# A graph layer on one core: A^T by block loads and score rows through DRAM, in place of TensorE transposes

## The chip, the cores and the metric

The kernel runs on one NeuronCore of a Trainium2 chip. The metric is the device time of one execution in microseconds (us), lower is better; the median of several runs counts. One execution was also recorded by the hardware profiler, and all views below come from it. PE is TensorE, PEld its weight load, DVE VectorE, ACT ScalarE, POOL GpSimd, SP the engine that only issues DMAs.

## The reference

There are 128 graphs of 128 nodes with 512 features, a weighted adjacency matrix A for each, and two layers.

```python
h = relu(layernorm(x))
sj, si = (h @ Wv + bv) @ aw[:512], (h @ Wv + bv) @ aw[512:]      # one number per node
e = leaky_relu(sj[:, None, :] + si[:, :, None] + ab, 0.2)
alpha = A * exp(e)
T = alpha / (sum(alpha, -1) + 1e-12)
x = x + relu(h @ Wk[0] + (T @ h) @ Wk[1] + (T @ T @ h) @ Wk[2] + bk.sum(0))

h = relu(layernorm(x))
q, k = split(h @ Wqk);  v = h @ Wv1
w = mask * sum(q * (A @ (k * mask)), -1) / sqrt(512)             # one number per node
x = x + softmax(w over the nodes)[:, :, None] * v
```

Two vectors of one number per node are needed along the free axis: sj, which is added to every row of e, and w, whose maximum and sum over all nodes are needed in every partition. A^T is needed as the stationary operand of the second layer's aggregation.

## The kernel before

A node is a partition. The kernel takes the graphs in pairs (`G = 2`), 64 of them (`NP`), with p counting the pairs; all data are fp32. The weights are folded in a setup: `score_matrix` makes one matrix of Wq and Wk, `attention_weights` folds Wv and aw into two vectors (`u_bc`), so that the scores are two weighted row sums of h.

Each layer multiplies the pair of graphs with its weights by one level of Strassen's scheme, seven products in place of eight: `strassen0` for layer 0 (the three hops stacked, L356 to L385) and `strassen1` for layer 1 (L387 to L409). Products are matmuls with a stationary operand of 128x128 (L346) into three banks of a PSUM pool of four; DVE adds the banks together between them. Results of other TensorE work go to a second pool of four banks (`ps_t`, tile `pt`).

A column of one number per node is turned into a row, the same in all partitions, by `spread` (L95 to L97): a TensorE transpose of the column broadcast to 128x128. A^T is a TensorE transpose too (L298), read out of PSUM by ACT with the mask as scale (L302). For h the kernel already goes another way: `by_blocks` (L258 to L266) stores h in DRAM and reads it back by four DMAs, so that 32x32 blocks lie in the right place, and `transposed` (L268 to L272) has DVE transpose every 32x32 block. SP issues these DMAs, and all others in the loop.

The steps of pair p, in the order of the text:

- `strassen0(p, steps)`: seven products; after the second, `steps[0]` runs `begin(p+1)` (block transposes of h into the operand x), `attention(p+1)` (L274 to L302: the score row, z, exp, the weighted sum with A, t = T, and A^T) and `end()`, which runs `finish` of pair p-2 (L426 to L445: the softmax over w, the last sum and the store). After the fourth product, `steps[1]` runs `t_transposed(p+1)` (L304 to L315: T^T, and (TT)^T by a matmul; ACT copies both out, L310 and L314).
- `propagate(p+1)`: T h and T T h, transposed (L325), copied out by ACT (L327).
- `norm_relu` of the first layer's result (L235 on ACT), its `by_blocks`.
- `strassen1(p-1)`, then `aggregate(p-1)` (L411 to L424: A k by L417 and the weighted row sum w by L420 on DVE).
- `prepare0(p+1)` and the block transposes and sums of layer 1's operand.
- `norm0(p+2)`, which loads pair p+3 (`load`, L68 to L73) and normalizes, and `score_sums(p+2)` (L248 to L256: four row sums on DVE, L255).

The instructions are not issued in just this order. The framework's planner orders each engine's queue ahead of the run, by the order of the text as priority and by its own costs of when an operand will be there; each queue then runs strictly in its order, and semaphores make it wait. A tile name with several buffers rotates; a new tile waits until the last reader of the old one is done. GpSimd's queue holds only a few set-up instructions.

Of the kernel before, what the change touches and what calls it, by code (L numbers as in the profile page):

```python
# [8 lines left out]
FP = mybir.dt.float32  # L9
# [6 lines left out]
def kernel(  # L16
# [27 lines left out]
    G = 2  # L44
# [20 lines left out]

    xg, ag = {}, {}

    def load(p):  # L68
        s = slice(p * G, (p + 1) * G)
        xg[p] = loads.tile([P, G, D], FP, name="xg")  # L70
        nc.sync.dma_start(xg[p], x[s].rearrange("b n d -> n b d"))
        ag[p] = loads.tile([P, G, N], FP, name="ag")
        nc.sync.dma_start(ag[p], adj[s].rearrange("b n m -> n b m"))  # L73


# [19 lines left out]
    def spread(dst, col):  # L95

        nc.tensor.transpose(dst, col.to_broadcast([P, P]), ident)  # L97
# [140 lines left out]

    H, HV, S, X, SX, AT, T, TT, X1, H2, X2, SX2 = ({} for _ in range(12))

# [7 lines left out]
    def score_sums(p):  # L248

        h = H[p]  # L250
        s = S[p] = small.tile([P, G, 2], FP, name="s")
        for j in range(G):
            for a in range(2):
                junk = front.tile([P, D], FP, name="junk", bufs=1)
                nc.vector.scalar_tensor_tensor(junk, h[:, j, :], 1.0, u_bc[:, a, :], op0=OP.mult,  # L255
                                               op1=OP.mult, accum_out=s[:, j, a:a + 1])  # L256

# [10 lines left out]
    def transposed(hv, dst):  # L268

        for j in range(G):  # L270
            nc.vector.transpose(dst[:, j].rearrange("p f (n b) -> p f n b", n=Q),  # L271
                                hv[:, j].rearrange("p n (f a) -> p f n a", f=Q))  # L272

    def attention(p):  # L274

        a, s = ag.pop(p), S.pop(p)
        pz = ps_t.tile([P, DC, P], FP, name="pt")
        for j in range(G):
            spread(pz[:, j, :], s[:, j, 0:1])
        z = front.tile([P, G, N], FP, name="z", bufs=1)  # L280
        for j in range(G):
            nc.vector.tensor_scalar(z[:, j, :], pz[:, j, :], s[:, j, 1:2], cz, op0=OP.add, op1=OP.add)
        nc.vector.scalar_tensor_tensor(z, z, 0.2, z, op0=OP.mult, op1=OP.max)
        ex = front.tile([P, G, N], FP, name="ex")
        nc.scalar.activation(ex, z, AF.Exp)
# [5 lines left out]
        nc.vector.reciprocal(d[:, 1], d[:, 0])  # L291
        t = T[p] = front.tile([P, G, N], FP, name="t")
        for j in range(G):
            nc.vector.tensor_scalar(t[:, j, :], ex[:, j, :], d[:, 1, j:j + 1], None, op0=OP.mult)

        pa = ps_t.tile([P, DC, P], FP, name="pt")
        for j in range(G):
            nc.tensor.transpose(pa[:, j, :], a[:, j, :], ident)  # L298
        AT[p] = front.tile([P, G, N], FP, name="aT", bufs=3)
        for j in range(G):  # L300
            b = p * G + j
            nc.scalar.activation(AT[p][:, j, :], pa[:, j, :], AF.Copy, scale=maskT[:, b:b + 1])  # L302

    def t_transposed(p):  # L304

        t, tt = T.pop(p), front.tile([P, G, 2, N], FP, name="tt")
        pt = ps_t.tile([P, DC, P], FP, name="pt")
# [48 lines left out]
    def strassen0(p, steps):  # L356
# [13 lines left out]
        steps[0]()  # L370
        product(bc, 7, True)
        product(bb, 5, False)
        nc.vector.tensor_add(s[:, 3], b, s[:, 0])
        nc.vector.tensor_add(hb[:, 1, HD:], c, s[:, 3])
        steps[1]()
        product(ba, 2, False)
        nc.vector.tensor_add(hb[:, 0, :HD], a, lo)
        product(bb, 3, False)
        nc.vector.tensor_add(hb[:, 0, HD:], b, s[:, 0])
# [6 lines left out]

    def strassen1(p):  # L387

# [12 lines left out]
        nc.vector.tensor_add(s[:, 2], b, s[:, 0])  # L401
        nc.vector.tensor_add(o[1][1], c, s[:, 2])
        product(a, 2, False)
        nc.scalar.copy(o[0][0], a)
# [6 lines left out]
    def aggregate(p, yv):  # L411

        h2, at = H2.pop(p), AT.pop(p)
        w = small.tile([P, 6, G], FP, name="w")
        for j in range(G):
# [6 lines left out]
                wscale[:, b:b + 1], yv[:, j, :, 0, :], op0=OP.mult, op1=OP.mult,  # L422
                accum_out=w[:, 0, j:j + 1])
        return w  # L424

    def finish(p, yv, w):  # L426

        pw = ps_t.tile([P, DC, P], FP, name="pt")
        for j in range(G):
            spread(pw[:, j, :], w[:, 0, j:j + 1])  # L430
        nc.vector.tensor_reduce(w[:, 1], pw[:, :G, :], AX.X, OP.max, negate=True)
        for j in range(G):
# [43 lines left out]
    for p in range(NP + 1):  # L476
        if p < NP:
            if p + 1 < NP:
                n = p + 1
                steps = (lambda: (begin(n), attention(n), end()), lambda: t_transposed(n))  # L480
            else:
                steps = (end, lambda: None)
            strassen0(p, steps)
            if p + 1 < NP:
                propagate(p + 1)
        else:
            end()
# [5 lines left out]
        if p < NP:  # L493
            H2[p] = norm_relu(X1[p], "h2", late["p"])
            hv2 = by_blocks(H2[p])
        if p > 0:
            yv = strassen1(p - 1)
            w = aggregate(p - 1, yv)
        if p + 1 < NP:
            prepare0(p + 1)  # L500
        if p > 0:
            ends.append((p - 1, yv, w))
        if p < NP:
# [4 lines left out]
            SX2[p] = left_sums(a, late["p"], "sx2", [1, HD])  # L508
        if p + 2 < NP:
            norm0(p + 2)  # L510
            score_sums(p + 2)
    end()
# [25 lines left out]
```

## Time and profile before

| | us |
|---|---|
| median of three runs | 2420.17 (2419.18 to 2420.50) |
| the profiled execution | 2420.37 |
| its span, first to last instruction | 2418.3 |
| one pair of graphs in the steady part | 36.70 |
| granted TensorE clock | 0.998 of full |

| group of instructions | count | mean ns |
|---|---|---|
| L346 products, 128x256 / 128x512 | 5376 / 1792 | 380 / 592 to 598 |
| L97 transposes of s, of w | 128, 128 | 276, 274 |
| L298 transposes of A | 128 | 275 |
| L271 DVE block transposes of 128x512 | 256 | 688 |
| L255 DVE score sums, 128x512 | 256 | 689 |
| L282 z from the score row in PSUM, 128x128 | 128 | 402 |
| L431 maximum over the row in PSUM, 128x256 | 64 | 414 |
| L302 ACT copy of A^T from PSUM, 128x128 | 128 | 363 |

The time of a matmul is from its start to its modelled end, and neighbours overlap, so the distance from start to start tells what one takes out of the time. A row of the stretches of time (used below) gives the stretch in us, its length, then for PE, PEld, DVE, ACT and POOL the busy us with the number of instructions, then the granted clock, the DMA engines' busy share and GB/s. DMA issues are not counted as busy. In the steady part the DMA engines are busy some 30% of the time; a DMA of 128 KB issued by SP takes some 3 us from issue to landing (`ag` 3.0, `hv` 3.3), one of 512 KB 3.1 to 3.6.

### The profile page before, as it was taken

To read this page: it belongs to the slowest core of one execution; us is meant where nothing else is said; L and a number is where in the kernel's file an instruction comes from. 1 tells how busy PE (TensorE), PEld (TensorE's weight loads), DVE (VectorE), ACT (ScalarE), POOL (GpSimd) and SP (SyncE) were. 2 spreads that over 40 slices of the span, in tenths; PEclk is the share of its full clock that TensorE was granted. 3 is DMA by queue.
4 is the path that set the end of the run, shared out by engine and by line. 5 is a ranking of instruction groups with operands and counts; after the bars stand their busy time and mean duration, and the time that the engine had idled before them with its cause. 6 is when DMAs were issued, how large, how long until landed. Compare 5 with 4: busy or idle time off the path is not lost.

```text
span 2418.3 us, 27245 instructions
## 1 busy us (share of the span) xinstructions
PE 2378.8 (98%) x9289; PEld 1694.5 (70%) x9289; DVE 1786.8 (74%) x4768; ACT 650.5 (27%) x1557; POOL 0.7 (0%) x6
## 2 busy tenths in 40 slices
PE   6999999999999999999999999999999999999997
PEld 4777677677676676776776776776766767767764
DVE  6777777777777777777777777777777777777764
ACT  3222222222222222223222222222222222232221
POOL 0000000000000000000000000000000000000000
PEclk9999999999999999999999999999999999999999
DMA  7233233233133233232332332332332332323311
GB/s 219 82 84 101 81 92 101 66 106 101 64 109 93 71 101 95 77 101 88 85 101 81 92 100 65 108 100 64 108 93 72 101 95 78 100 87 86 97 52 52
DMA packets 236986, 220.48 MB, mean 91 GB/s; under 512 B 14384, under 2 KB 170160, under 8 KB 236848
## 3 DMA queue, kind: packets, MB, share of 16 engines
q1 hardware_dynamic: 232624, 216.65, 30.5%
q10 hardware_dynamic: 4224, 2.10, 0.3%
q8 instruction: 73, 1.20, 0.2%
q14 instruction: 65, 0.53, 0.1%
HBM read 118.03 MB, written 100.66 MB: 90 GB/s over the span
## 4 chain that ended last, share of the span: by engine, by line
PE 96%; DVE 2%; DMA 1%; issue 0%; ACT 0%; SPq 0%; DVEq 0%; ACTq 0%
PE pm L346 79%; PE pt L325 9%; PE pt L417 4%; PE pt L97 1%; PE pt L313 1%; PE pt L298 1%; PE pt L309 1%; DMA bk_bc<-in_L_gnn_bk_dram 0%; DMA hd<-h 0%; DVE st L220 0%; DMA hv<-hd 0%; DMA w<-in_L_gnn_Wqk_dram 0%; DMA xg<-in_x_dram 0%; DVE x L271 0%; PE pm L208 0%
## 5 line engine op out<-in xcount | busy, mean ns | idle before, releaser
L346 PE MATMUL pm<-t,sx 128*128 128x256 f32 x2304 | 518.6, 380 | 1.4 <-DVE sx L333 1.4
L346 PEld LDWEIGHTS pm<-t,sx 128*128 128x128 f32 x2304 | 433.4, 190 | 57.4 <-DVE sx L333 2.0
L346 PE MATMUL pm<-b,x 128*128 128x256 f32 x1536 | 363.0, 380 | 0.0
L346 PE MATMUL pm<-f,sx 128*128 128x512 f32 x768 | 344.8, 598 | 0.3
L346 PEld LDWEIGHTS pm<-b,x 128*128 128x128 f32 x1536 | 282.6, 191 | 59.3 <-issue 29.6
L327 ACT COPY x<-pt 128x512 f32<-128x512 f32 x256 | 148.7, 581 | 500.6 <-PE pt L325 500.6
L346 PEld LDWEIGHTS pm<-f,sx 128*128 128x128 f32 x768 | 141.6, 191 | 193.7 <-issue 154.4
L346 PE MATMUL pm<-e,x 128*128 128x512 f32 x512 | 242.5, 596 | 6.5 <-DVE x L271 6.5
L325 PE MATMUL pt<-tt,h 128*128 128x256 f32 x1024 | 231.5, 379 | 0.0
L325 PEld LDWEIGHTS pt<-tt,h 128*128 128x128 f32 x1024 | 194.9, 190 | 26.2
L255 DVE SCALAR_TENSOR_TENSOR junk<-h,u_bc 128x512 f32<-128x512 f32 x256 | 176.4, 689 | 7.8 <-ACT h L235 0.9
L346 PE MATMUL pm<-b,sx 128*128 128x256 f32 x768 | 176.5, 379 | 0.0
L346 PE MATMUL pm<-t,x 128*128 128x256 f32 x768 | 176.2, 379 | 0.0
L235 ACT ACTIVATE h<-x,rs 128x512 f32<-128x512 f32 x128 | 97.2, 806 | 289.9 <-PE pt L417 277.1
L271 DVE STREAM_TRANSPOSE x<-hv 128x512 f32<-128x512 f32 x256 | 166.4, 688 | 6.6 <-DMA hv<-hd 5.7
L346 PEld LDWEIGHTS pm<-e,x 128*128 128x128 f32 x512 | 97.8, 191 | 102.8 <-issue 92.3
L346 PEld LDWEIGHTS pm<-t,x 128*128 128x128 f32 x768 | 146.2, 190 | 19.6
L346 PEld LDWEIGHTS pm<-b,sx 128*128 128x128 f32 x768 | 146.0, 190 | 19.5
L406 DVE TENSOR_TENSOR yv<-pm,s 128x512 f32<-128x512 f32 x64 | 44.3, 692 | 128.5 <-PE pm L346 128.5
L235 ACT ACTIVATE h<-xg,rs 128x512 f32<-128x512 f32 x128 | 97.2, 806 | 119.8 <-DVE rs L232 119.8
L417 PE MATMUL pt<-h,aT 128*128 128x512 f32 x256 | 120.5, 593 | 0.5 <-ACT h L235 0.5
L346 PE MATMUL pm<-e,sx 128*128 128x512 f32 x256 | 120.3, 592 | 0.0
(101 smaller groups left out, 2511.3 us busy)
## 6 DMA issues: line engine op xcount, KB each, us to landing
hd<-h SPq DMA_DIRECT2D x128, 512.0 KB, 3.1
hv<-hd SPq DMA_DIRECT2D x512, 128.0 KB, 3.3
xg<-in_x_dram SPq DMA_DIRECT2D x64, 512.0 KB, 3.6
out_dram<-x SPq DMA_DIRECT2D x64, 512.0 KB, 3.1
ag<-in_adj_dram SPq DMA_DIRECT2D x64, 128.0 KB, 3.0
w<-in_L_gnn_Wqk_dram ACTq DMA_DIRECT2D x8, 256.0 KB, 5.0
b<-in_L_gnn_Wk_dram SPq DMA_DIRECT2D x8, 256.0 KB, 3.4
wv_sb<-in_L_gnn_Wv_dram SPq DMA_DIRECT2D x4, 256.0 KB, 5.3
```

Source lines behind the costliest of these rows:

```text
L97: nc.tensor.transpose(dst, col.to_broadcast([P, P]), ident)
L235: nc.scalar.activation(h[:, j, :], src[:, j, :], AF.Relu, bias=rs[:, 1, j:j + 1], scale=rs[:, 0, j:j + 1])
L255: nc.vector.scalar_tensor_tensor(junk, h[:, j, :], 1.0, u_bc[:, a, :], op0=OP.mult, op1=OP.mult, accum_out=s[:, j, a:a + 1])
L271: nc.vector.transpose(dst[:, j].rearrange("p f (n b) -> p f n b", n=Q), hv[:, j].rearrange("p n (f a) -> p f n a", f=Q))
L298: nc.tensor.transpose(pa[:, j, :], a[:, j, :], ident)
L309: nc.tensor.transpose(pt[:, j, :], t[:, j, :], ident)
L313: nc.tensor.matmul(pt[:, j, :], t[:, j, :], tt[:, j, 0, :], start=True, stop=True)
L325: nc.tensor.matmul(pt[:, c].rearrange("p k n -> p (k n)"), h[:, j, at:at + P], tt[:, j].rearrange("p k n -> p (k n)"), start=True, stop=True)
L327: nc.scalar.copy(X[p][:, 1:3, j, kh].rearrange("p k c n -> p c k n"), pt)
L346: nc.tensor.matmul(bank[:, :r.shape[-1]], left[i][:, k, c * P:(c + 1) * P], r, start=(first and at == 0), stop=(at == len(chunks) - 1), sk ...
L406: nc.vector.tensor_add(o[0][1], b, s[:, 0])
L417: nc.tensor.matmul(pa, at[:, j, :], h2[:, j, :], start=True, stop=True)
```

## The change

It touches how two kinds of rows and A^T come about, and where some steps stand.

- A^T: `load` also reads A by four DMAs issued by GpSimd into `agb`, with the 32x32 blocks in their transposed places; `attention` has DVE transpose the blocks into `aT`, and ACT scales `aT` in place.
- Rows: the new `spread_pair` takes a 32-column tile whose first columns are the values of the two graphs. DVE transposes its 32x32 blocks, GpSimd writes the row of each graph to DRAM (two DMAs) and reads both back broadcast to all partitions (one DMA). The score row of pair 0 and the weight row of the last pair keep the TensorE transposes. s and w now live in six fixed 32-column tiles, cleared once.
- Places: `strassen0` has four steps in place of two: `begin` after the second product, `attention` after the third, `end` after the fourth and its sums, `t_transposed` after the fifth. `norm0(p+2)` stands ahead of `strassen1(p-1)`, and `score_sums(p+2)` within it, after the fourth product; the score row's DMAs are issued there, the weight row's where `end` is prepared.
- Buffers: `ex` is the tile `z`, and `t` and `tt` have one buffer each.

```diff
--- before.py
+++ after.py
@@ -63,7 +63,7 @@
 
         return bass.AP(tensor=ap.tensor, offset=ap.offset + offset, ap=[[0, P], [1, n]])
 
-    xg, ag = {}, {}
+    xg, ag, agb = {}, {}, {}
 
     def load(p):
         s = slice(p * G, (p + 1) * G)
@@ -71,6 +71,10 @@
         nc.sync.dma_start(xg[p], x[s].rearrange("b n d -> n b d"))
         ag[p] = loads.tile([P, G, N], FP, name="ag")
         nc.sync.dma_start(ag[p], adj[s].rearrange("b n m -> n b m"))
+        agb[p] = loads.tile([P, G, Q, S32], FP, name="agb", bufs=2)
+        v = adj[s].rearrange("g (q b) (c i) -> c b (g q) i", b=S32, i=S32)
+        for c in range(Q):
+            nc.gpsimd.dma_start(agb[p][c * S32:(c + 1) * S32].rearrange("p g q i -> p (g q) i"), v[c])
 
 
     nc.scalar.preload_act_table_set("natural_log_exp_and_others")
@@ -236,7 +240,10 @@
                                  bias=rs[:, 1, j:j + 1], scale=rs[:, 0, j:j + 1])
         return h
 
-    H, HV, S, X, SX, AT, T, TT, X1, H2, X2, SX2 = ({} for _ in range(12))
+    cols = [const.tile([P, S32], FP, name=f"col{i}") for i in range(6)]
+    for t in cols:
+        nc.gpsimd.memset(t, 0.0)
+    H, HV, S, PZ, X, SX, AT, T, TT, X1, H2, X2, SX2 = ({} for _ in range(13))
 
     def norm0(p):
 
@@ -248,12 +255,13 @@
     def score_sums(p):
 
         h = H[p]
-        s = S[p] = small.tile([P, G, 2], FP, name="s")
+        s = S[p] = cols[p % 3]
         for j in range(G):
             for a in range(2):
                 junk = front.tile([P, D], FP, name="junk", bufs=1)
                 nc.vector.scalar_tensor_tensor(junk, h[:, j, :], 1.0, u_bc[:, a, :], op0=OP.mult,
-                                               op1=OP.mult, accum_out=s[:, j, a:a + 1])
+                                               op1=OP.mult, accum_out=s[:, a * G + j:a * G + j + 1])
+        PZ[p] = spread_pair(s, "pz", p > 0)
 
     def by_blocks(h):
 
@@ -271,17 +279,31 @@
             nc.vector.transpose(dst[:, j].rearrange("p f (n b) -> p f n b", n=Q),
                                 hv[:, j].rearrange("p n (f a) -> p f n a", f=Q))
 
+    def spread_pair(col, name, by_dma):
+
+
+        if by_dma:
+            t = small.tile([P, S32], FP, name=f"{name}t", bufs=1)
+            nc.vector.transpose(t, col)
+            d = dram.tile([G, Q, S32], FP, name=f"{name}d")
+            for j in range(G):
+                nc.gpsimd.dma_start(d[j], t[j::S32])
+            dst = front.tile([P, G, N], FP, name=name, bufs=1)
+            nc.gpsimd.dma_start(dst.rearrange("p g n -> p (g n)"), bcast(d, 0, G * N))
+            return dst
+        pz = ps_t.tile([P, DC, P], FP, name="pt")
+        for j in range(G):
+            spread(pz[:, j, :], col[:, j:j + 1])
+        return pz[:, :G]
+
     def attention(p):
 
-        a, s = ag.pop(p), S.pop(p)
-        pz = ps_t.tile([P, DC, P], FP, name="pt")
-        for j in range(G):
-            spread(pz[:, j, :], s[:, j, 0:1])
+        a, s, pz = ag.pop(p), S.pop(p), PZ.pop(p)
         z = front.tile([P, G, N], FP, name="z", bufs=1)
         for j in range(G):
-            nc.vector.tensor_scalar(z[:, j, :], pz[:, j, :], s[:, j, 1:2], cz, op0=OP.add, op1=OP.add)
+            nc.vector.tensor_scalar(z[:, j, :], pz[:, j, :], s[:, G + j:G + j + 1], cz, op0=OP.add, op1=OP.add)
         nc.vector.scalar_tensor_tensor(z, z, 0.2, z, op0=OP.mult, op1=OP.max)
-        ex = front.tile([P, G, N], FP, name="ex")
+        ex = z
         nc.scalar.activation(ex, z, AF.Exp)
         d = small.tile([P, 2, G], FP, name="d")
         for j in range(G):
@@ -289,21 +311,20 @@
                                            op1=OP.mult, accum_out=d[:, 0, j:j + 1])
         nc.vector.tensor_scalar(d[:, 0], d[:, 0], 1e-12, None, op0=OP.add)
         nc.vector.reciprocal(d[:, 1], d[:, 0])
-        t = T[p] = front.tile([P, G, N], FP, name="t")
+        t = T[p] = front.tile([P, G, N], FP, name="t", bufs=1)
         for j in range(G):
             nc.vector.tensor_scalar(t[:, j, :], ex[:, j, :], d[:, 1, j:j + 1], None, op0=OP.mult)
 
-        pa = ps_t.tile([P, DC, P], FP, name="pt")
-        for j in range(G):
-            nc.tensor.transpose(pa[:, j, :], a[:, j, :], ident)
         AT[p] = front.tile([P, G, N], FP, name="aT", bufs=3)
+        nc.vector.transpose(AT[p].rearrange("p g n -> p (g n)"),
+                            agb.pop(p).rearrange("p g q i -> p (g q i)"))
         for j in range(G):
             b = p * G + j
-            nc.scalar.activation(AT[p][:, j, :], pa[:, j, :], AF.Copy, scale=maskT[:, b:b + 1])
+            nc.scalar.activation(AT[p][:, j, :], AT[p][:, j, :], AF.Copy, scale=maskT[:, b:b + 1])
 
     def t_transposed(p):
 
-        t, tt = T.pop(p), front.tile([P, G, 2, N], FP, name="tt")
+        t, tt = T.pop(p), front.tile([P, G, 2, N], FP, name="tt", bufs=1)
         pt = ps_t.tile([P, DC, P], FP, name="pt")
         for j in range(G):
             nc.tensor.transpose(pt[:, j, :], t[:, j, :], ident)
@@ -369,12 +390,14 @@
         nc.vector.tensor_add(s[:, 2], b, s[:, 1])
         steps[0]()
         product(bc, 7, True)
+        steps[1]()
         product(bb, 5, False)
         nc.vector.tensor_add(s[:, 3], b, s[:, 0])
         nc.vector.tensor_add(hb[:, 1, HD:], c, s[:, 3])
-        steps[1]()
+        steps[2]()
         product(ba, 2, False)
         nc.vector.tensor_add(hb[:, 0, :HD], a, lo)
+        steps[3]()
         product(bb, 3, False)
         nc.vector.tensor_add(hb[:, 0, HD:], b, s[:, 0])
         product(bc, 4, False)
@@ -384,7 +407,7 @@
             nc.vector.scalar_tensor_tensor(hb[:, j, :], hb[:, j, :], 0.0, xs[:, j, :],
                                            op0=OP.max, op1=OP.add)
 
-    def strassen1(p):
+    def strassen1(p, ahead):
 
         product = products(SX2.pop(p), R1)
         X2.pop(p)
@@ -400,6 +423,8 @@
         product(b, 5, False)
         nc.vector.tensor_add(s[:, 2], b, s[:, 0])
         nc.vector.tensor_add(o[1][1], c, s[:, 2])
+        if ahead < NP:
+            score_sums(ahead)
         product(a, 2, False)
         nc.scalar.copy(o[0][0], a)
         product(b, 3, False)
@@ -411,7 +436,7 @@
     def aggregate(p, yv):
 
         h2, at = H2.pop(p), AT.pop(p)
-        w = small.tile([P, 6, G], FP, name="w")
+        w = cols[3 + p % 3]
         for j in range(G):
             pa = ps_t.tile([P, D], FP, name="pt")
             nc.tensor.matmul(pa, at[:, j, :], h2[:, j, :], start=True, stop=True)
@@ -420,15 +445,13 @@
             nc.vector.scalar_tensor_tensor(
                 junk.rearrange("p (k d) -> p k d", k=2), pa.rearrange("p (k d) -> p k d", k=2),
                 wscale[:, b:b + 1], yv[:, j, :, 0, :], op0=OP.mult, op1=OP.mult,
-                accum_out=w[:, 0, j:j + 1])
+                accum_out=w[:, j:j + 1])
         return w
 
-    def finish(p, yv, w):
-
-        pw = ps_t.tile([P, DC, P], FP, name="pt")
-        for j in range(G):
-            spread(pw[:, j, :], w[:, 0, j:j + 1])
-        nc.vector.tensor_reduce(w[:, 1], pw[:, :G, :], AX.X, OP.max, negate=True)
+    def finish(p, yv, ws, pw):
+
+        w = ws[:, :6 * G].rearrange("p (k g) -> p k g", g=G)
+        nc.vector.tensor_reduce(w[:, 1], pw, AX.X, OP.max, negate=True)
         for j in range(G):
             ej = front.tile([P, N], FP, name="ej")
             nc.scalar.activation(ej, pw[:, j, :], AF.Exp, bias=w[:, 1, j:j + 1],
@@ -477,9 +500,9 @@
         if p < NP:
             if p + 1 < NP:
                 n = p + 1
-                steps = (lambda: (begin(n), attention(n), end()), lambda: t_transposed(n))
+                steps = (lambda: begin(n), lambda: attention(n), end, lambda: t_transposed(n))
             else:
-                steps = (end, lambda: None)
+                steps = (lambda: None, lambda: None, end, lambda: None)
             strassen0(p, steps)
             if p + 1 < NP:
                 propagate(p + 1)
@@ -493,22 +516,24 @@
         if p < NP:
             H2[p] = norm_relu(X1[p], "h2", late["p"])
             hv2 = by_blocks(H2[p])
+        if p + 2 < NP:
+            norm0(p + 2)
         if p > 0:
-            yv = strassen1(p - 1)
+            yv = strassen1(p - 1, p + 2)
+        elif p + 2 < NP:
+            score_sums(p + 2)
+        if p > 0:
             w = aggregate(p - 1, yv)
         if p + 1 < NP:
             prepare0(p + 1)
         if p > 0:
-            ends.append((p - 1, yv, w))
+            ends.append((p - 1, yv, w, spread_pair(w, "pw", p < NP)))
         if p < NP:
             X2[p] = late["p"].tile([P, G, 2, HC, N], FP, name="x2")
             transposed(hv2, X2[p].rearrange("p j h c n -> p j (h c) n"))
             a = {(j, kh): X2[p][:, j, kh:kh + 1].rearrange("p k c n -> p k (c n)")
                  for j in range(G) for kh in range(2)}
             SX2[p] = left_sums(a, late["p"], "sx2", [1, HD])
-        if p + 2 < NP:
-            norm0(p + 2)
-            score_sums(p + 2)
     end()
```

More of the change, by code (lines that the diff above doesn't have):

```diff
@@ L272, in transposed, with attention @@
                                 hv[:, j].rearrange("p n (f a) -> p f n a", f=Q))
-    def attention(p):
-        a, s = ag.pop(p), S.pop(p)
+    def spread_pair(col, name, by_dma):
[8 more added lines that the diff above has]
+            return dst
         pz = ps_t.tile([P, DC, P], FP, name="pt")
         for j in range(G):
-            spread(pz[:, j, :], s[:, j, 0:1])
+            spread(pz[:, j, :], col[:, j:j + 1])
+        return pz[:, :G]
+    def attention(p):
+        a, s, pz = ag.pop(p), S.pop(p), PZ.pop(p)
         z = front.tile([P, G, N], FP, name="z", bufs=1)
         for j in range(G):
-            nc.vector.tensor_scalar(z[:, j, :], pz[:, j, :], s[:, j, 1:2], cz, op0=OP.add, op1=OP.add)
+            nc.vector.tensor_scalar(z[:, j, :], pz[:, j, :], s[:, G + j:G + j + 1], cz, op0=OP.add, op1=OP.add)
         nc.vector.scalar_tensor_tensor(z, z, 0.2, z, op0=OP.mult, op1=OP.max)
-        ex = front.tile([P, G, N], FP, name="ex")
+        ex = z
         nc.scalar.activation(ex, z, AF.Exp)
```

## The prediction

> **What bounds the kernel now.** I read the table of busy time first, then the chain that ended last, then who TensorE waited for, then one steady stretch of TensorE in order of time.
>
> ```profile
> PE 2378.8 (98%) x9289; PEld 1694.5 (70%) x9289; DVE 1786.8 (74%) x4768; ACT 650.5 (27%) x1557; POOL 0.7 (0%) x6
> ...
> PE 96%; DVE 2%; DMA 1%; issue 0%; ACT 0%; SPq 0%; DVEq 0%; ACTq 0%
> PE pm L346 79%; PE pt L325 9%; PE pt L417 4%; PE pt L97 1%; PE pt L313 1%; PE pt L298 1%; PE pt L309 1%; DMA bk_bc<-in_L_gnn_bk_dram 0%; DMA hd<-h 0%; DVE st L220 0%; DMA hv<-hd 0%; DMA w<-in_L_gnn_Wqk_dram 0%; DMA xg<-in_x_dram 0%; DVE x L271 0%; PE pm L208 0%
> ```
>
> A busy share alone would not do, as matmuls overlap. But 96% of the chain is TensorE, and its listed waits add up to some 32 us, nearly all at the start and the end. So any TensorE time taken out of the loop shortens the kernel, as long as nothing new makes TensorE wait. GpSimd does nothing. The next view is TensorE in order of time, columns start, duration, line, operation and count:
>
> ```profile
> 1214.56 2.75 PE L346 MATMUL pm<-b,x 128*128 128x256 f32 x12
> 1217.15 2.75 PE L346 MATMUL pm<-t,sx 128*128 128x256 f32 x12
> 1219.74 0.38 PE L97 MATMUL pt<-ident,s 128*128 128x128 f32 x2
> 1219.95 0.38 PE L298 MATMUL pt<-ident,ag 128*128 128x128 f32 x2
> 1220.17 0.38 PE L97 MATMUL pt<-ident,w 128*128 128x128 f32 x2
> 1220.39 5.35 PE L346 MATMUL pm<-t,sx 128*128 128x256 f32 x24
> ```
>
> The six transposes start at 1219.74 and the next product at 1220.39: 0.65 us for six, **0.108 us each**. The mean of one in the groups of instructions, 275 ns, is a latency; what leaves the time is the pitch. The last view counts busy time in two stretches one pair of graphs long:
>
> ```profile
> 1177.86:1214.56 36.70, 36.70 (x146) 26.26 (x145) 27.23 (x75) 10.01 (x24) 0.00 (x0) 1.00 0.30 90
> 1214.56:1251.26 36.70, 36.70 (x146) 26.26 (x145) 27.94 (x75) 10.01 (x24) 0.00 (x0) 1.00 0.29 90
> ```
>
> A pair takes 36.70 us, TensorE is busy in all of it, DVE in 27 to 28, ACT in 10, the DMA engines in 30%.
>
> **What the Trainium skill says.** "TensorE: Matmul & The Clock Gate", Part 4, gives about 275 ns for a 128x128 transpose in a kernel, mostly access latency; the trace agrees (273 to 276 ns), and its pitch shows that this is not the cost. "VectorE: DVE Perf Modes", The three transpose paths, says DVE transposes 32x32 blocks only, not a whole 128x128; so the blocks must be placed by DMA, as `hv<-hd` and L271 already do (688 ns for 512 columns). "DMA: Bandwidth & Descriptors", SWDGE vs HWDGE vs iDMA, says that a DMA issued by GpSimd has its descriptors written by software; no GpSimd DMA is in this trace. "SBUF — State Buffer", Who interferes with whom, says DVE in a two-port mode blocks GpSimd; the candidates here are short tensor_scalars (L294, 280 ns), too short to matter.
>
> **The change, part by part.**
> *Removed from TensorE.* Score rows for pairs 1 to 63, attention-weight rows for pairs 0 to 62, A^T for pairs 1 to 63 (pair 0 is in the setup, where TensorE waits anyway): 3 x 63 x 2 = 378 transposes x 0.108 = **40.9 us less**.
> *Added to DVE.* L271 gives 688 ns for 512 columns; other rows give 419 ns for 256 and 951 for 768, so some 155 ns fixed and 1.04 ns a column. The A^T transpose of 256 columns is then 0.42 us, the two 32-column ones 0.19 each: 0.80 us a pair. z (402 ns from PSUM) and the maximum (414) now read SBUF; I count nothing. DVE goes from 27.6 to 28.4 of 36.05 us: not a bound. The scaling of A^T on ACT stays (363 ns). Both are covered by TensorE.
> *Added to GpSimd's queue.* Per pair: four block loads of 32 KB each in pieces of 128 B, and for each of two rows two writes of 512 B and one broadcast of 128 KB: ten DMAs. Nothing else stands on that queue. The skill's DMA page (Anatomy of one DMA — SWDGE path) prices one at about 2.0 us and bytes/436e3, with about 1 us until its first byte. Ten cost 10 us of issue, or 20 if each held the queue for its whole 2.0: both fit in 36. The price of 256 small pieces per block load is open. Low end: 1 us. High end: with six row DMAs at 2.0, four loads fill the pair at (36.05-12)/4 = 6.0 us each. I take 2. DMA traffic grows by 0.39 MB on 3.4 MB a pair, 11%, of engines 30% busy: hidden; the queue of SP gains nothing.
> *Moved.* The norm of pair p+2 and its score sums go ahead of and into the second Strassen. With it go the norm's store of h and four reads back on SP, and its x and adj loads; SP's long waits at the norms' store (L261, 1070 us in total) show that those stand idle until ACT delivers, so earlier is harmless. The four sums take 3.1 us of DVE; its idle times before L406 and L408, 2.0 and 1.0 us a pair, take them in. L406 and L408 behind them can be up to 3 us late: the bank that L406 reads is next written by the third product of the next pair's first Strassen, at 1219.74, over 5 us later.
>
> *New wait one, the score row.* Sums end near 1209.3 + 3.1 = 1212.4 on the clock of the stretch above; block transpose 0.2; second write 1.0 + 2.0, broadcast 2.0 + 0.3: ready at 1217.9. It is due where attention must start so that t (its DVE chain took 1220.28 to 1224.2, and 0.42 for A^T) is there for the transposes that now follow product 2, 1227.5: at about 1223. Slack **5 us**. Behind the waiting z stand L373 and L374, needed by products 3 and 4.
> *New wait two, the weight row.* w is complete at about 1216.0 (L420); the same chain of 5.5 us makes it 1221.5. Waiting for it is the maximum (L431), and behind that on DVE L377 and L443; on ACT the two exponentials (L434), and behind them, in the order of the text, the copy L310 of t^T, for which TensorE waits at L313. L313 comes near 1228.6; less 0.37, 1.11 and 0.41 for those three, the row is due at 1226.6. Slack **5 us** again. Without that cover, L313 is late next.
> *Buffers.* ex shares z, and t and tt have one buffer. Each is last read by the pair before (propagate ended at 1200.9; t is transposed 37 us apart), so these cost nothing.
> *Setup and end.* Block loads for two or three pairs join a first 50 us where DMA moves 230 GB/s: 0.13 MB each, 0.6 us each; between 0 and 2 us, I take 1. The last pair stays on TensorE: nothing.
>
> *Sum.* The profiled execution took 2420.37 us (span 2418.3), the median of the runs is 2420.17, 0.2 less. -40.9 + 1.0 = -39.9: 2380.5 for the execution, **2380 us** for the median.
>
> **Rivals.**
> *Small stalls eat part of it.* Slacks of 5 us on two guessed chains may be passed in some pairs by tenths. Each 0.1 us a pair is 6.3 us: 2386 to 2415. For it: neither chain was seen. Against: the slack is nearly as long as the chain.
> *GpSimd's in-order queue becomes the bound (slower).* Place: the broadcast of the weight row, near 1219 to 1222, while the four block loads become ready near 1224 when attention gives up its buffer. If the queue's order puts them in front, or if a block load takes well over 2 us, the row comes behind 8 us or more of issue: 8 - 5 = 3 us of wait at L313 in each of 63 pairs, +190, so 2380 + 190 = 2570; at a chain 2 us over the slack, 2380 + 126 = 2506. It decides from 0.65 us past the slack, a row chain of about 11 us in place of 5.5. A longer TensorE gap costs more: after the 6.5 us wait near the end, four matmuls of 512 columns took 3.78 us instead of 1.88. For it: software descriptors, small pieces, one queue. Against: ten priced DMAs fill half the pair, and w is complete 8 us ahead of the next freed buffer.
> *The change does not shorten TensorE.* If the six slots were filled by waiting that remains (weight loads, L373), the time stays 2420. Against: the products before and after run at the same pitch of 0.216 us and no wait is listed.
>
> **How the numbers follow.** About 0.2% (4.8 us) is what a measurement of this kernel can tell from no change. Full gain 0.60, part of it 0.10, no change 0.04, queue as bound 0.26. Faster 0.70, same 0.04, slower 0.26. The prediction is the full gain, 2380. Its own range is 2376 (no cost in the setup, earlier starts) to 2386. To hold 8 in 10 the range must take in partial gain, no change and the milder part of the slower rival (stalls up to 1.6 us a pair, 100 us): 2376 to 2480.
>
> **What would show it.** Right: the period of a pair is 36.05 us with TensorE busy in all of it; the `ident` rows of s and ag nearly gone and no new TensorE wait; DVE waits at z or L431 for a DMA at most tenths of a us. Wrong: TensorE waits for L310 at L313, or for DVE L373 at product 3; ACT waits at L434 for L431, and L431 for the pw broadcast; GpSimd issues fill over 30 us of a pair, with the row DMAs behind the block loads; landing times of row DMAs over 5 us.

## The result and the profile after

The changed kernel takes **2696.7 us** (median of four runs, 2687.78 to 2702.58) against 2419.68 for the kernel before on the same chip: a ratio of **1.114, 95% interval 1.1108 to 1.1175**. The forecast was 2380 with a range to 2480. The direction is that of the slower rival; the time lies beyond even that rival's 2570. Line numbers below are those of the changed kernel unless another is named: the sums L373 and L374 of before are now L395 and L396, the maximum L431 is L454, the exponentials L434 are L457, the copies L310 and L314 are L331 and L335, the matmul L313 is L334.

The table of busy time on the page of the changed kernel:

```profile
PE 2450.2 (91%) x8909; PEld 1735.9 (64%) x8909; DVE 1803.6 (67%) x4958; ACT 647.4 (24%) x1557; POOL 371.2 (14%) x646
```

TensorE runs 380 matmuls and transposes fewer than before, and yet it is busy for longer, and for 91% of the span instead of 98%. GpSimd, which the slower rival suspected, is busy 14% (on GpSimd this profile does count the issue of a DMA as busy). A stretch of about one pair in the steady part (us, length, then busy us and instructions of PE, PEld, DVE, ACT and POOL, clock, DMA share, GB/s):

```profile
1218.00:1259.00 41.00, 37.91 (x140) 27.06 (x139) 27.84 (x78) 9.96 (x25) 5.88 (x10) 0.96 0.33 90
```

A pair takes about 41 us instead of 36.70. TensorE stands idle for 3 us of it, and the granted clock is 0.96 instead of 1.00. GpSimd's ten DMAs keep it for 5.9 us. From the distance between the first aggregations of successive pairs: 118.98 us to the first one (before 111.51), then 61 steady pairs of 41.10 us on average (36.71), then the end. So +7.5 us at the start, +267.7 in the steady part, +4.6 at the end: +279.8 of span. Nearly all of the loss is 4.4 us in each pair.

The waits of the changed kernel (engine, line, what released it: us in total, times, longest):

```profile
ACT ej L457 <- DVE col L454: 475.2, 64, 10.0
DVE col L454 <- DMA pw<-pwd: 335.5, 63, 10.0
...
PE pm L367 <- DVE s L395: 190.1, 61, 4.6
DVE z L304 <- DMA pz<-pzd: 57.1, 63, 4.6
...
PE pm L367 <- DVE s L390: 5.0, 3, 2.7
```

TensorE waits for the sum L395 in 61 pairs, 3.1 us each. DVE in its turn waits 5.3 us a pair for the weight row's broadcast. The DMA issues (KB each, median us from issue to landing) show how long the new ones take:

```profile
hd<-h SPq DMA_DIRECT2D x128, 512.0 KB, 4.6
hv<-hd SPq DMA_DIRECT2D x512, 128.0 KB, 3.7
agb<-in_adj_dram POOLq DMA_DIRECT2D x256, 32.0 KB, 4.1
pz<-pzd POOLq DMA_DIRECT2D x63, 128.0 KB, 3.3
pw<-pwd POOLq DMA_DIRECT2D x63, 128.0 KB, 4.4
pzd<-pzt POOLq DMA_DIRECT2D x126, 0.5 KB, 1.6
pwd<-pwt POOLq DMA_DIRECT2D x126, 0.5 KB, 4.8
```

The two rows are written by the same code with the same sizes. The score row's 512 bytes land in 1.6 us, the weight row's in 4.8. The store of h takes 4.6 us, before it took 3.1. One pair in order of time (start, us, engine, line, operation) shows why, and how it reaches TensorE:

```profile
1229.99 1.16 POOL L290 DMA_DIRECT2D pzd<-pzt  x2 [28.95 <-DVE pzt L287]
...
1232.76 0.58 POOL L292 DMA_DIRECT2D pz<-pzd  x1 [1.61 <-DMA pzd<-pzt]
...
1233.19 0.17 DVE L287 STREAM_TRANSPOSE pwt<-col 128x32 f32<-128x32 f32 x1
...
1233.56 0.62 POOL L77 DMA_DIRECT2D agb<-in_adj_dram  x1 [0.23 <-DVE pwt L287]
1233.62 0.88 SPq L269 DMA_DIRECT2D hd<-h  x2
1234.18 1.14 POOL L290 DMA_DIRECT2D pwd<-pwt  x2
...
1237.67 4.11 SPq L273 DMA_DIRECT2D hv<-hd  x8
...
1239.96 0.58 POOL L292 DMA_DIRECT2D pw<-pwd  x1 [2.83 <-DMA pwd<-pwt]
...
1244.66 0.42 DVE L454 TENSOR_REDUCE col<-pw 128x2 f32<-128x256 f32 x1 [5.10 <-DMA pw<-pwd]
...
1246.49 1.41 DVE L466 SCALAR_TENSOR_TENSOR x<-yv,col,x 128x512 f32<-128x512 f32 x2
1247.82 0.42 DVE L395 TENSOR_TENSOR s<-pm,s 128x256 f32<-128x256 f32 x1
...
1248.30 2.08 PE L367 MATMUL pm<-b,sx 128*128 128x256 f32 x4 [3.10 <-DVE s L395]
1250.16 1.06 PE L334 MATMUL pt<-tt,t 128*128 128x128 f32 x4
```

The last term of w is written at 1232.91. One block load's issue (0.62) stands ahead of the row's writes. They are issued at 1234.18, half a microsecond after SP has sent off two stores of 512 KB, and their landing is seen only at 1239.96. The broadcast leaves amid eight reads of 128 KB and arrives at 1244.66, **11.75 us after w**. Behind the waiting maximum stand the rest of the softmax, the last sum L466 and then L395, which was ready to run since product 5 ended near 1242.2. TensorE, which needs the bank that L395 frees, waits 3.10 us, and then its four products of 256 columns take 2.08 us instead of 1.03, the four of 128 columns 1.06 instead of 0.61.

### The profile page after: what moved, and what is told of

Read it like the earlier page. It is cut to its first block, busy times and chain, and to the rows that moved or that the text cites. A ratio compares the mean times of both kernels' runs of the same rounds, so it can differ in the third digit from the quotient of the medians.

```text
span 2698.1 us, 27592 instructions
## 1 busy us (share of the span) xinstructions
PE 2450.2 (91%) x8909; PEld 1735.9 (64%) x8909; DVE 1803.6 (67%) x4958; ACT 647.4 (24%) x1557; POOL 371.2 (14%) x646
## 5 line engine op out<-in xcount | busy, mean ns | idle before, releaser
L367 PE MATMUL pm<-t,sx 128*128 128x256 f32 x2304 | 508.6, 379 | 6.6 <-DVE s L390 5.0
L367 PE MATMUL pm<-b,sx 128*128 128x256 f32 x768 | 275.0, 512 | 190.1 <-DVE s L395 190.1
L367 PE MATMUL pm<-b,x 128*128 128x256 f32 x1536 | 352.6, 379 | 0.0
L367 PEld LDWEIGHTS pm<-b,sx 128*128 128x128 f32 x768 | 191.0, 265 | 235.6 <-DVE s L395 204.8
L367 PEld LDWEIGHTS pm<-b,x 128*128 128x128 f32 x1536 | 291.8, 190 | 66.1 <-issue 29.7
L290 POOL DMA_DIRECT2D pzd<-pzt x126 | 72.6, 578 | 1893.5 <-DVE pzt L287 1883.8
L454 DVE TENSOR_REDUCE col<-pw 128x2 f32<-128x256 f32 x63 | 26.5, 420 | 335.5 <-DMA pw<-pwd 335.5
L457 ACT ACTIVATE ej<-pw,col 128x128 f32<-128x128 f32 x126 | 49.5, 394 | 470.0 <-DVE col L454 470.0
L77 POOL DMA_DIRECT2D agb<-in_adj_dram x256 | 154.1, 607 | 30.4 <-DVE pwt L287 17.0
```

Of the source, the lines that this page charges most:

```text
L77: nc.gpsimd.dma_start(agb[p][c * S32:(c + 1) * S32].rearrange("p g q i -> p (g q) i"), v[c])
L290: nc.gpsimd.dma_start(d[j], t[j::S32])
L367: nc.tensor.matmul(bank[:, :r.shape[-1]], left[i][:, k, c * P:(c + 1) * P], r, start=(first and at == 0), stop=(at == len(chunks) - 1), sk ...
L454: nc.vector.tensor_reduce(w[:, 1], pw, AX.X, OP.max, negate=True)
L457: nc.scalar.activation(ej, pw[:, j, :], AF.Exp, bias=w[:, 1, j:j + 1], accum_out=w[:, 2, j:j + 1])
```

## The experiments

Three explanations had to be told apart: the block loads, in GpSimd's queue and on the DMA engines, hold up the weight row; the row's chain through DRAM is late by itself or by something else; the place of the waiting maximum in DVE's queue makes a loss of what would be harmless. All ratios are to runs of the kernel before on the same chip (2418 to 2421 us).

### A^T alone

The kernel before, with only the A^T part of the change:

```diff
+        agb[p] = loads.tile([P, G, Q, S32], FP, name="agb", bufs=2)
...
+            nc.gpsimd.dma_start(agb[p][c * S32:(c + 1) * S32].rearrange("p g q i -> p (g q) i"), v[c])
...
-            nc.tensor.transpose(pa[:, j, :], a[:, j, :], ident)
+        nc.vector.transpose(AT[p].rearrange("p g n -> p (g n)"),
+                            agb.pop(p).rearrange("p g q i -> p (g q i)"))
```

> Only A^T goes by block loads and a DVE block transpose; both rows stay TensorE transposes in their old places, and ex shares z's tile. It takes 126 transposes of 0.108 us, 13.6 us, off TensorE. Theory (the weight row comes late, the A^T path is innocent): 2406 to 2412 us, no new TensorE wait. Rival (the block loads themselves cost, by their small pieces or by what they do to the other DMAs): above 2430.

Measured: 2408.27 us, **0.9952 (0.9937 to 0.9967)**. All but two steady pairs take 36.48 us, 0.22 less than before: two transposes at 0.108. A stretch of 100 us in the middle:

```profile
1200.00:1300.00 100.00, 100.00 (x394) 71.64 (x393) 74.14 (x205) 25.89 (x63) 6.90 (x12) 1.00 0.34 98
```

TensorE is busy in all of it, so block loads and DVE's transpose hide, as expected. The first aggregation comes 1.6 us later.

### The weight row back on TensorE

The changed kernel, with the weight row again by TensorE in `finish`:

```diff
-            ends.append((p - 1, yv, w, spread_pair(w, "pw", p < NP)))
+            ends.append((p - 1, yv, w, None))
...
+        if pw is None:
+            pw = spread_pair(ws, "pw", False)
```

> The changed kernel, with the weight row alone back on two TensorE transposes at the place where the softmax starts. Theory (all of the loss comes from the weight row's way through DRAM): 252 transposes stay away, 27 us, less some 5 to 8 us of setup and end: 2395 to 2401 us, with no wait at the first sum after product 5. Rival (score row or A^T also delay the loop): above 2430.

Measured: 2412.24 us, **0.9967 (0.9954 to 0.998)**. The whole loss is gone with the weight row, but the time is 11 us over what was expected. Pairs take 36.20 us, except three of 40.04, 40.27 and 42.95, and the first aggregation comes at 118.18 instead of 111.51. In the waits the three show:

```profile
PE pm L367 <- DVE s L390: 7.8, 3, 3.8
```

L390 is the sum after product 1; it stands behind the z that waits for the score row. In the longest of these pairs the second of the score row's two writes was issued at 1538.37 and landed only at 1542.12, 3.75 us later, although SP's stores of h left after 1541.5; the broadcast that waited for it then fell into these stores. Why this one write was slow was not settled.

### No block loads

The changed kernel, with A^T by TensorE again and both rows still by DMA:

```diff
-        agb[p] = loads.tile([P, G, Q, S32], FP, name="agb", bufs=2)
...
-            nc.gpsimd.dma_start(agb[p][c * S32:(c + 1) * S32].rearrange("p g q i -> p (g q) i"), v[c])
...
+            nc.tensor.transpose(pa[:, j, :], a[:, j, :], ident)
```

> The changed kernel without block loads: A^T is again a TensorE transpose, both rows go through DRAM. Theory A (block loads in GpSimd's queue make the weight row late): the row's writes are issued 0.8 us earlier and land in about 1.6 us like the score row's instead of 4.7, the row is there 4 us earlier, no TensorE wait, 2393 to 2402 us. Theory B (the stores and reads of h on SP's queue, issued at the same moment, delay the row): the writes still take over 4 us, the row stays 1 to 3 us late, and the time is 2520 to 2680.

Measured: 2545.13 us, **1.0528 (1.0506 to 1.0549)**. The weight row is still late with nothing but the rows in GpSimd's queue:

```profile
pw<-pwd POOLq DMA_DIRECT2D x63, 128.0 KB, 4.2
pzd<-pzt POOLq DMA_DIRECT2D x126, 0.5 KB, 1.6
pwd<-pwt POOLq DMA_DIRECT2D x126, 0.5 KB, 3.9
```

TensorE waits 100.7 us for the same sum (L392 here), 1.65 us a pair instead of 3.1. So the block loads are not the whole cause: without them 125 of the 277 us of loss remain. But they matter: 1.5 us of the wait in a pair goes with them.

### Block loads issued by SP

```diff
-            nc.gpsimd.dma_start(agb[p][c * S32:(c + 1) * S32].rearrange("p g q i -> p (g q) i"), v[c])
+            nc.sync.dma_start(agb[p][c * S32:(c + 1) * S32].rearrange("p g q i -> p (g q) i"), v[c])
```

> The changed kernel with the same block loads issued by SP instead of GpSimd. Theory A (order in GpSimd's own queue and rings): the row is early enough, 2380 to 2390 us. Theory B (contention with whatever else moves at that moment): the row's writes still take over 4 us to land, 2520 to 2690.

Measured: 2609.34 us, **1.0784 (1.0766 to 1.0801)**. The waits for L395 are 135.6 us in 59 pairs, 2.3 each, and the row's writes and its broadcast both land in 4.2 us. Freeing GpSimd's queue takes off 0.8 us of the 3.1; the 0.65 us that remain above the run without block loads go with the loads' transfers or with their place in SP's queue, which this run does not tell apart.

### The maximum behind the sums on DVE

The changed kernel, with `end` held behind the sum L396 (`issue_after` binds the order of the queue to it):

```diff
-        nc.vector.tensor_add(hb[:, 1, HD:], c, s[:, 3])
-        steps[2]()
+        last = nc.vector.tensor_add(hb[:, 1, HD:], c, s[:, 3])
+        with tc.issue_after(last.ins):
+            steps[2]()
```

> The changed kernel; only DVE's queue differs: the end of the pair two back (the maximum L454 over the weight row and what follows) may not stand ahead of the two sums after product 5 (L395, L396). The row comes as late as before. Theory (the loss is head-of-line waiting on DVE: the sum L395 stands behind the maximum that waits for the row): TensorE no longer waits at product 3; the exponentials still stand ahead of the copy of t^T on ACT, so up to 0.4 us a pair may be waited there: 2385 to 2412 us. Rival (the wait only moves to the next engine that stands behind the row, ACT): above 2500.

Measured: 2503.93 us, **1.0343 (1.0326 to 1.036)**. The row is as late as before (writes 4.9, broadcast 4.6 us), and the wait for L395 has left the list:

```profile
PE pt L334 <- ACT tt L331: 42.3, 49, 1.8
...
PE pm L367 <- DVE s L422: 15.6, 57, 0.6
```

Now the exponentials wait on ACT, and the copy L331 behind them makes TensorE wait at L334, 0.86 us in 49 pairs. This is the wait that the prediction had named; it was expected to be 0.4 us. So the wait at L395 is explained, but the time of this theory was missed and the rival's was met. Pairs take 36 to 40 us, 37.9 on average, 1.9 more than without any wait (36.0, worked out below). From start to start of TensorE's matmuls 0.8 us of this is lost at L334, and another 0.8 among the products of the second layer, half of it at the sum L422, half in small gaps whose cause is open. The first aggregation comes at 124.5.

### The maximum and the exponentials both later

The same, with `end` behind the sum after product 2 on DVE, and the exponentials behind the copy L331 on ACT:

```diff
-        nc.vector.tensor_add(hb[:, 0, :HD], a, lo)
-        steps[3]()
+        last = nc.vector.tensor_add(hb[:, 0, :HD], a, lo)
+        copied = steps[3]()
+        with tc.issue_after(last.ins):
+            end(copied)
...
+            with tc.issue_after(copied.ins) if copied is not None else ExitStack():
```

> The changed kernel, with the end step behind the sum of product 2 on DVE, and its exponentials behind the first copy of t^T on ACT. The row comes as late as in the changed kernel. Theory: nothing that TensorE needs stands behind the row, the pair takes 36.0 us, and with 5 to 8 us more in the setup the time is 2380 to 2388 us. Rival (the late row, or the traffic of the block loads, hurts elsewhere too): above 2400.

Measured: 2439.05 us, **1.0075 (1.0057 to 1.0093)**. The row is no earlier (writes 5.0, broadcast 4.8 us), but 258 of the 277 us are gone, and most pairs take 36.52 us:

```profile
PE pm L368 <- DVE s L424: 16.0, 60, 0.3
...
PE pm L368 <- DVE s L391: 9.2, 5, 4.2
```

So the late row costs little where the work behind it on DVE and ACT is not needed soon. Still over 50 us more than the theory expected, and the rival's "hurts elsewhere too" holds: 0.5 us in most pairs, most of it (0.42 from start to start) at a new wait for L424 in the second layer; five waits behind z, which take some pairs to 39 and once to 43.5 us; and 5 us at the end (the 5.7 at the start had been expected).

### No stores of h

The kernel without block loads; h is not stored, and the block reads take x from the input, so that the products are made of other numbers:

```diff
-        hd = dram.tile([G, P, D], FP, name="hd")
-        nc.sync.dma_start(hd.rearrange("g n d -> n g d"), h)
+        hd = x[p * G:(p + 1) * G]
```

> The kernel of the run without block loads, and in addition h is not stored to DRAM: the block reads take x from its input in place of h, so the products are of other numbers. Theory B (the row's writes and the broadcast wait behind the 512 KB stores of h that leave at the same moment): the writes land in about 1.6 us as the score row's do, the broadcast in about 3.3, the row is 3 us earlier and TensorE waits no more: 2393 to 2405 us. Rival (the writes are slow of themselves): they still take near 4 us and the time stays above 2500.

Measured: 2566.16 us, **1.0612 (1.0595 to 1.0629)**. This does not decide: the reads no longer wait for a store, so they move ahead into the moment of the row. Four of them leave at 1206.36, the row's writes at 1207.73. The writes take 4.5 us as before. It was one bulk transfer in place of another.

### The weight row alone

The kernel without block loads, with the score row on TensorE too, so that the weight row's three DMAs are all that GpSimd issues in the loop:

```diff
-        PZ[p] = spread_pair(s, "pz", p > 0)
+        PZ[p] = None
...
+        pz = spread_pair(s, "pz", False)
```

> The kernel of the run without block loads, with the score row on TensorE as well, so that the weight row is the only thing on GpSimd's queue. Theory B1 (its writes wait for SP's stores of h, issued at the same moment): landing near 4 us as before, TensorE waits as before, 2530 to 2570 us. Theory B2 (its writes wait behind the score row's broadcast of 128 KB in the same queue): landing 1.6 to 2.5 us, no wait, 2405 to 2415 us.

Measured: 2817.3 us, **1.1646 (1.1627 to 1.1666)**. The weight row in the order of time:

```profile
1238.44 1.11 POOL L286 DMA_DIRECT2D pwd<-pwt  x2 [37.91 <-DVE pwt L283]
1238.61 0.88 SPq L265 DMA_DIRECT2D hd<-h  x2
...
1241.63 3.79 SPq L269 DMA_DIRECT2D hv<-hd  x8
...
1243.53 0.57 POOL L288 DMA_DIRECT2D pw<-pwd  x1 [3.98 <-DMA pwd<-pwt]
...
1247.73 0.42 DVE L452 TENSOR_REDUCE col<-pw 128x2 f32<-128x256 f32 x1 [5.06 <-DMA pw<-pwd]
```

The queue is empty ahead of it, and yet the second write lands 4 us after its issue and the broadcast comes 4.2 us after its own. That a score row broadcast in front of it is needed to hold it up is therefore refuted. The time is worse because the planner now put the maximum ahead of the whole attention, z to t, on DVE, so that TensorE waits for t:

```profile
PE pt L328 <- DVE t L313: 249.0, 61, 5.8
```

### No traffic of h

The kernel without block loads; the blocks of h are read once at the start and kept, so that neither its stores nor its reads are in the loop, and the products are made of other numbers:

```diff
+    hvs = []
...
+        if hvs:
+            return hvs[0]
+        hv = const.tile([P, G, Q, P], FP, name="hv")
```

> The kernel of the run without block loads, both rows through DRAM; h makes no way through DRAM at all: the blocks of one pair of x are loaded once and used in place of h's, so the products are of other numbers. Theory B1 (SP's traffic of h): the weight row's writes land in about 1.6 us, the broadcast in about 3.3, no wait, 2393 to 2405 us. Theory B2 (the score row's broadcast ahead in GpSimd's queue): landing still near 4 us, TensorE waits 1 to 2 us a pair, above 2490 us.

Measured: 2396.54 us, **0.9906 (0.9891 to 0.9921)**, against 1.0528 with that traffic. Most pairs take 36.20 us:

```profile
pw<-pwd POOLq DMA_DIRECT2D x63, 128.0 KB, 3.2
pzd<-pzt POOLq DMA_DIRECT2D x126, 0.5 KB, 1.6
pwd<-pwt POOLq DMA_DIRECT2D x126, 0.5 KB, 1.6
```

The weight row's writes are as quick as the score row's, and the broadcast loses 1 us; only six pairs still wait for the sum, 1 us each. So what makes the row late in the kernel without block loads is that it shares the moment with SP's stores and reads of h. From the end of its block transpose to the landing of its broadcast the row takes 6.3 us here (median), 10.2 with the traffic of h, and 11.2 in the changed kernel, with the block loads as well.

### A repaired version

The changed kernel, with the weight row on TensorE, the score row by DMA from pair 2, and attention's DVE work held behind the sum L390:

```diff
-        PZ[p] = spread_pair(s, "pz", p > 0)
+        PZ[p] = spread_pair(s, "pz", p > 1)
...
+        with tc.issue_after(last.ins):
+            steps[1]()
...
+            ends.append((p - 1, yv, w, None))
```

> The changed kernel with the weight row on TensorE, the score row through DRAM from pair 2 on (pair 1 on TensorE), and the attention on DVE behind the sum after product 6. Theory (in the run with the weight row on TensorE three pairs were late because that sum stood behind the wait for the score row, and the setup was late because of pair 1's row): every pair takes 36.2 us, 2390 to 2398 us. Rival (the late pairs and the setup have another cause): 2403 to 2416 us as in that run.

Measured: 2399.01 us, **0.9915 (0.990 to 0.993)**, the best of all that leave nothing out: 20 us less than the kernel before on the same chip (2419.01). The late pairs are gone; nearly all take 36.20 us:

```profile
1300.00:1400.00 100.00, 100.00 (x379) 69.98 (x378) 74.47 (x211) 28.11 (x68) 12.35 (x21) 1.00 0.38 100
```

The start is still late (first aggregation at 119.26), so pair 1's row alone is not what delays it.

## Why the prediction was wrong

**Right: the gain.** 0.108 us for each transpose. A^T alone gave 0.22 us a pair, A^T and the score row 0.50 (four would be 0.43; the other 0.07 is a gap between two products of the second layer that TensorE had in every pair before, and that the repaired version doesn't have). **Right: the new work on DVE and GpSimd.** A^T's block transpose takes 0.44 us (0.42 worked out), the small ones 0.17 to 0.20 (0.19). A GpSimd issue takes 0.57 to 0.62 us, below the 1 to 2 assumed, for the block loads' 256 small pieces too. **Right: that the score row is covered, though its chain was mis-sized.** Its writes and broadcast land in 1.6 and 3.3 us. From its block transpose on it takes 6.3 us (median) where 5.3 was worked out, mostly by the broadcast; the slack takes this in, and apart from three waits in this profile it costs the steady part nothing.

**Wrong: the weight row's chain, "the same chain of 5.5 us".** It measured 11.75 us. Step by step, on the pair shown: the small transpose is done 0.45 after w (0.2), a block load's issue and the gap before it take 0.82 (0), two issues 1.14 (1.0), landing 4.64 (2.0), the broadcast with its issue 4.70 (2.3). Four fifths of the 6.25 us that were missed lie in the landing and the broadcast. By the three medians given with the experiment on the traffic of h, some 1 us is missing from the price even in quiet, 3.9 us go with that traffic and 1.0 with the block loads. The step "DMA traffic ... hidden" made the error: a mean share of 30% says nothing of the moment. The profile before shows the moment, in SP's queue and in the busy share of the DMA engines:

```profile
1216.30 0.88 SPq L261 DMA_DIRECT2D hd<-h  x2
1219.11 3.82 SPq L265 DMA_DIRECT2D hv<-hd  x8
```

```profile
1217.50:1224.00 6.50, 6.50 (x35) 5.76 (x34) 5.57 (x23) 1.83 (x8) 0.00 (x0) 1.00 0.89 278
```

w is complete at 1215.95 there, and both stores of h leave 0.35 us later, when the second layer's h is ready. From 1217.5 to 1224 the DMA engines are busy 89% of the time (the last but one number of the row), and the prediction put its row from 1216.2 to 1221.5. Moving the norm neither made this nor undid it: the norm's h is ready at 1225.78 in the pair shown after, but its store still leaves together with that of the second layer, at 1233.62, as in all 61 steady pairs of both kernels. So SP's long waits at L261, which the prediction read as room for an earlier store of the norm, end in the steady part with the second layer's h.

That the row shares its way with these transfers, the Trainium skill says: "DMA: Bandwidth & Descriptors", Issuing engines are not separate DMA queues, has DMAs of all issuing engines interleave on the same 16 DMA engines, and Latency and other measured facts puts the HBM latency, the main part of a small DMA's fixed cost, at 0.2 us on average and 2 us at high load. The runs agree and go further: 1.6 us quiet, 3.9 beside the traffic of h, 4.8 with the block loads as well.

**Wrong: the due time, "the row is due at 1226.6".** That is 10.6 us after w. The prediction put L377 and L443 of before behind the waiting maximum and took the order of the text for L373. The planner put the maximum ahead of that sum. In the pair shown TensorE was ready at 1245.20, and from the start of the maximum to TensorE's start go 3.64 us, so the maximum was due at 1241.56: 8.65 us after w. Slack: 8.65 - 11.75 = -3.1 instead of +5.1. With the maximum where the prediction thought it to be (the maximum behind the sums on DVE), the wait at the matmul it had named came, and it was 0.86 us on average.

**Mis-sized: the price of a wait.** A pair without any wait would take about 36.0 us: 36.70 less six transposes (0.65) and the 0.07 above. Against 41.10 that is 5.1 us, of which the wait is 3.1. By pairs of the changed kernel and the two that differ in the block loads, set out by the length of their wait: up to 1.75 us of wait (45 pairs) a pair grows by the wait and a steady 0.26; from 1.85 us on some, from about 2.7 us on nearly all grow by the wait and 1.93. The steady 0.26 is lost around the wait: a listed wait counts from the modelled end of the transpose before it, which lies 0.16 us behind the pitch, and the second matmul after the wait comes 0.10 late. The 1.67 us between 0.26 and 1.93 is TensorE at half pace for some 3.4 us, as the timeline above shows. "TensorE: Matmul & The Clock Gate", Part 1, describes such a half rate, after an idle window of about 3.4 us and for about as long; here waits of 2.7 us nearly always sufficed, some of 1.85 too. The prediction had seen the half pace after a 6.5 us wait but added nothing for it to 190 us of waits. With 1.93 x 61 = 118 us its rival would have come to 2688.

**The rival "GpSimd's in-order queue becomes the bound"** had the right row, stretch and deciding point ("a row chain of about 11 us"), and the wrong mechanism: the queue has room (5.9 of 41 us), only one 0.62 us issue stood in front of the row's writes, and without any block load the kernel is still 5% slower. That its 190 us of waits is what was measured at L395 is luck: it came of 8 us of issues less a slack of 5, at another matmul. Its argument against, that w is complete 8 us ahead of the next freed buffer, did not hold either: DVE's block transpose of A^T frees the buffer at 1233.27, 0.36 us after w. A rival built on the transfers that leave in the same moment was not considered.

**Mis-sized: start and end.** Taken at +1 and 0, measured +7.5 and +4.6. With A^T alone the start is 1.6 us later; without block loads it is 121.25, and with the score row on TensorE as well 111.77, as before, so the score row's way takes part in it. But without stores of h it came at 111.83 and without any traffic of h at 118.33, with the score row by DMA in both, so it is not that alone, and what makes it was not settled. The end's delay goes with the weight row by DMA (35.4 us from the last aggregation before, 40.2 after, 35.9 with that row on TensorE).

**Still open.** Whether the row's writes are held on the DMA engines or at the memory was not tried; that the engines are 89% busy in that stretch doesn't decide it. How much the block loads alone would cost, without the traffic of h, was not run. Nor is it known why the second layer's sums come late in the two runs with a bound order.

## What to carry to other kernels

Price a small DMA on a critical chain by what leaves in the same few microseconds, not by the mean share of the DMA engines: find in the timeline the bulk transfers released by the same event, and move the one or the other (no run here tried this move; the repaired version took the row off the DMA path). Before an instruction is made to wait on such a chain, look at what the planner puts behind it on its in-order queue, and bind the order where something urgent stands there. In this kernel a TensorE wait that comes in every iteration cost more than its length once it exceeded some 2 us.

## What the runs showed of the hardware

- A 512-byte write from SBUF to DRAM issued by GpSimd lands in 1.6 us when little else moves, and in 3.2 to 5.0 us (medians of the runs) where two stores of 512 KB leave at the same moment, with eight reads of 128 KB behind them.
- A DMA issue on GpSimd takes some 0.6 us (0.57 to 0.62), for a row of four pieces or a block of 256.
- TensorE waits up to 1.75 us left its pace alone; nearly all over 2.7 us cost a further 1.67 us.
